# Two transformer layers in one launch: padded keys cleared on another engine, layer norms in two halves, another order of tiles in SBUF, scatters behind the first decays

## The chip, the cores and the metric

The kernel runs on one core of a Trainium2 chip. The engines of that core work side by side, each with an instruction queue taken strictly in order: PE (TensorE, matrix products and transposes, with PEld for its weight loads), DVE (VectorE), ACT (ScalarE), POOL (GpSimd) and SP (SyncE, which here only issues DMAs). POOL issues DMAs too: those that convert types, and the indirect ones that gather or scatter rows. Semaphores tie the queues together. SBUF is the memory on the chip, PSUM the small one that PE writes to. The metric is the time of one launch in microseconds (us) on the device.

## The reference, cut to what matters

T = 1024 tokens of width D = 256 go through two layers. Each is a layer norm, a token mixer, a mixture of experts, and a residual sum of the mixer times the gated experts.

```python
x = L0_attn_x
xn = _layernorm(x, axis=-1)
s = _L0_attn_ref(xn, wq, wk, wv, wo)            # 32 heads of width 8, 8 kv heads, causal softmax
g = _silu(_L0_ffn_ref(xn, gate, gate_up, down)) # 32 experts, 4 per token
x = x + s * g
xn = _layernorm(x, axis=-1)
s = _L1_attn_ref(xn, W_qkv, W_z, W_b, W_a, conv_w, dt_bias, A_log, norm_w, W_out)
g = _silu(_L1_ffn_ref(xn, Wr, Wg, Wu, Wd))      # 8 experts, 2 per token
x = x + s * g

def _layernorm(x, axis=-1, eps=1e-05):
    m = jnp.mean(x, axis=axis, keepdims=True)
    v = jnp.var(x, axis=axis, keepdims=True)
    return (x - m) / jnp.sqrt(v + eps)

# inside _L1_attn_ref: a gated delta rule over time, 32 value heads on 16 key heads of width 128
S = S * jnp.exp(gt)[..., None, None]
kS = jnp.einsum('bhk,bhkv->bhv', kt, S)
S = S + bt[..., None, None] * kt[..., :, None] * (vt - kS)[..., None, :]
o = jnp.einsum('bhk,bhkv->bhv', qt, S)
```

## The kernel before, in words

Tokens lie in NT = 8 tiles of 128. The kernel is written with a tile framework: pools of named tiles, and a scheduler that orders each engine's instructions by priority (program order, shifted by `high_priority`) over a simulated time. A pool that takes the place of an earlier one comes after it. In the first layer's main loop the orders of PE and SP are written out by hand; elsewhere the scheduler decides.

**First layer, `l0_block`.** Pool `l0c` holds what lives through the layer, placed in the order in which the code names it: `qp`, `kp`, `vaug`, `ytok`, `maskm`, `xn` (later `fo`), `logits`, the padded queries `qaugs`, keys `kaug` and `kzs`, then `xr`, `wo` and the plan. `kzs` are two tiles of [128, 4, 1024] that hold each head's keys in 32 rows of their own with zeros around them; POOL clears them once (L272), and SP later writes the rows (L408). `layer_norm` (L74) takes statistics of all eight tiles on DVE (L79, L80), then one reciprocal square root of all (L81, `rsqrt` at L50: eleven small DVE instructions), then scales all eight (L84). `transpose_split` (L87) turns `xn` on PE, four tiles at a time, with ACT keeping the rounded high part (L95) and DVE the rest (L96); its outer loop runs over the two halves of D, its inner loop over the two halves of T. Then eight projections of three product terms each (`mm3`, L69 to L71) with copies by ACT (L284 to L287). The weights come in raw by SP and rounded by POOL (`split_weights`, L47, L48), and POOL subtracts (L49). `moe.clear` (L135) fills the experts' input `l0xs` in DRAM with zeros from the tile `zero`. The loop then runs row maxima (L421, L423, L427), attention (L487, L491, L493) and expert blocks; the experts' results are gathered row by row by POOL (L222), and the tail (from L540) forms `x1` (L548 to L551).

**Second layer, `l1_block`.** Its constants are in pool `l1c`: `xnh` and `xnl` of 8 KB a partition each, then `tri_l`, `cw` and small ones. SP stores `x1` (L602) and loads `cw` (L610), `nw` (L613), clears `l1xs` (L135), loads `dt`, `ea` and the weights `wba` of the gates (L47). Layer norm and transposes follow (L1107, L1109), the products `ba` (L1118), the decays' exponents, and the routing plan (`Blocks.plan`), whose tiles lie in pool `l1a`. Pool `mp` (four `m` tiles) takes the place of `l1a`. Eight groups of heads follow, as generators that a string of letters steps through: K, Q, V are projections with a convolution on DVE (L681) and SiLU on ACT; P (`pre`) makes the eight decays of a group (`decay`: POOL selects `b` at L729, PE L731, ACT exp L733; then PE `pkk` L751, DVE products L762 into `m`, POOL select L771) and inverts the triangular blocks (DVE L791 and L793, then PE and ACT); R is the recurrence (L874 to L923); O the output (L964 to L983); F the expert blocks, which hold one `m` tile and one `v` tile from their first to their twelfth block. P has a priority 3000 instructions ahead of its place. `table` ties exps and SiLUs of ACT into windows.

Before the string `START` is run, eight loads `xt` (SP, L1160, from the stored `xn`; four buffers `kd`, which R uses too) and sixteen indirect DMAs on POOL (`moe.scatter`, L215) put the tokens into the experts' input `l1xs`. The sixteen scatters wait for the plan's `to` (L200).

Of the kernel before, what the change touches and what calls it, by code (L numbers as in the profile page):

```python
# [8 lines left out]
F32 = mybir.dt.float32  # L9
FR = mybir.dt.float32r  # L10
BF = mybir.dt.bfloat16
AF = mybir.ActivationFunctionType
ALU = mybir.AluOpType
# [6 lines left out]
T, D = 1024, 256  # L20
NT = T // 128
KT = D // 128


def f32(ap):
    return ap.bitcast(F32)
# [26 lines left out]
def rsqrt(nc, pool, out, x, n):  # L53

    I32 = mybir.dt.int32
    y = pool.tile([128, n], F32, tag="rsy", name="rsy")
    t = pool.tile([128, n], F32, tag="rst", name="rst")
    nc.vector.tensor_scalar(t.bitcast(I32), x.bitcast(I32), 1, None, ALU.logical_shift_right)
    nc.vector.tensor_scalar(y.bitcast(I32), t.bitcast(I32), -1.0, float(0x5F3759DF), ALU.mult, ALU.add)
    for i in range(3):  # L60
        nc.vector.tensor_tensor(t, y, y, ALU.mult)
        nc.vector.scalar_tensor_tensor(t, t, -0.5, x, ALU.mult, ALU.mult)
        nc.vector.scalar_tensor_tensor(out if i == 2 else y, t, 1.5, y, ALU.add, ALU.mult)
# [10 lines left out]
def layer_norm(nc, c, pool, x, xn):  # L74
    st = pool.tile([128, NT, 6], F32, tag="lnst", name="lnst")
    mv = pool.tile([128, NT, 2], F32, tag="lnmv", name="lnmv")
    rs = pool.tile([128, NT], F32, tag="lnrs", name="lnrs")
    for t in range(NT):
        nc.vector.bn_stats(st[:, t, :], x[:, t, :])  # L79
        nc.vector.bn_aggr(mv[:, t, :], st[:, t, :])  # L80
    nc.vector.tensor_scalar(rs, mv[:, :, 1], 1e-5, None, ALU.add)  # L81
    rsqrt(nc, pool, rs, rs, NT)
    for t in range(NT):
        nc.vector.tensor_scalar(xn[:, t, :], x[:, t, :], mv[:, t, 0:1], rs[:, t : t + 1], ALU.subtract, ALU.mult)  # L84


def transpose_split(nc, c, ps, tag, xn, hi, lo):  # L87

    for k in range(KT):
        for h in range(2):  # L90
            p = ps.tile([128, 4, 128], F32, tag=tag, name="ptr")
            for j in range(4):
                nc.tensor.transpose(p[:, j, :], xn[:, 4 * h + j, k * 128 : (k + 1) * 128], c.ident)
            sl = slice(512 * h, 512 * h + 512)
            nc.scalar.copy(hi[:, k, sl], p.rearrange("p a b -> p (a b)"))  # L95
            nc.vector.tensor_tensor(lo[:, k, sl], p.rearrange("p a b -> p (a b)"), f32(hi[:, k, sl]), ALU.subtract)  # L96
# [23 lines left out]
class Blocks:  # L120
# [91 lines left out]
    def scatter(self, tc, t, x):  # L212

        for k in range(self.K):
            ins = self.nc.gpsimd.indirect_dma_start(out=self.xs[:, :], out_offset=bass.IndirectOffsetOnAxis(ap=self.to[:, t, k : k + 1], axis=0),  # L215
                                                    in_=x, in_offset=None).ins
            for other in self.scatters:
                tc.declare_no_dep(ins, other, reason="different rows")
            self.scatters.append(ins)

    def gather(self, t, k, y):
        self.nc.gpsimd.indirect_dma_start(out=y, out_offset=None, in_=self.ys[:, :],  # L222
# [3 lines left out]
def l0_block(ctx, tc, c, x_d, wq, wk, wv, wo, gate, gup, dproj, x1, dbg=None):  # L226
    nc = tc.nc
# [4 lines left out]
    const = ctx.enter_context(tc.tile_pool(name="l0c", bufs=1))  # L232
    small = ctx.enter_context(tc.tile_pool(name="l0s", bufs=2))

    qp = const.tile([128, NT, 256], F32, name="qp")
    kp = const.tile([128, NT, 64], F32, name="kp")
    vaug = const.tile([128, NT, NKV, 32], F32, name="vaug")
# [4 lines left out]
    logits = const.tile([128, NT, NE], F32, name="logits")  # L242
    dram = ctx.enter_context(tc.tile_pool(name="l0d", bufs=1, space=bass.MemoryType.DRAM))
    moe = Blocks(nc, dram, "l0", NE, 4, per=2)
    qaugs = [const.tile([128, NT, 4, 32], FR, tag=f"qaug{i}", name=f"qaug{i}") for i in range(2)]
    kaug = const.tile([128, NT, 4, 32], FR, tag="kaug", name="kaug")


    kzs = [const.tile([128, 4, T], FR, tag=f"kz{i}", name=f"kz{i}") for i in range(2)]
    for q in qaugs:  # L250
        nc.vector.memset(f32(q), 0.0)
    nc.vector.memset(f32(kaug), 0.0)
# [4 lines left out]
    with tc.tile_pool(name="l0a", bufs=1) as pa, tc.tile_pool(name="l0ap", bufs=2, space=PSUM) as pp:  # L257
        x = pa.tile([128, NT, D], F32, name="x")
        xnh = pa.tile([128, KT, T], FR, name="xnh")
        xnl = pa.tile([128, KT, T], FR, name="xnl")  # L260
        zero = pa.tile([128, D], F32, name="zero")
        nc.vector.memset(zero, 0.0)
        nc.sync.dma_start(x, x_d.rearrange("(t p) d -> p t d", p=128))
        NW = NH * HD + 2 * NKV * HD + NE
        loads = []
        off = 0
        for w, n in ((wq, 256), (wk, 64), (wv, 64), (gate, 32)):
            loads.append((lambda t, o=off, n=n: t[:, :, o : o + n], w.rearrange("(k p) n -> p k n", p=128)))
            off += n
        wh, wl = split_weights(nc, pa, "wqkv", [128, KT, NW], loads)  # L270
        for kz in kzs:
            nc.gpsimd.memset(f32(kz), 0.0)  # L272
        layer_norm(nc, c, small, x, xn)
        transpose_split(nc, c, pp, "ptr", xn, xnh, xnl)
        nc.gpsimd.memset(maskm, 0.0)

        nc.gpsimd.affine_select(maskm, maskm, [[-1, 896]], ALU.is_ge, -1e30, base=384, channel_multiplier=1)
        moe.clear(zero)
        for t in range(NT):
            p = pp.tile([128, NW], F32, tag="pq", name="pq")  # L280
            for k in range(KT):
                ts = slice(t * 128, t * 128 + 128)
                mm3(nc, p, (xnh[:, k, ts], xnl[:, k, ts]), (wh[:, k, :], wl[:, k, :]), k == 0, k == KT - 1)
            nc.scalar.copy(qp[:, t, :], p[:, 0:256])  # L284
            nc.scalar.copy(kp[:, t, :], p[:, 256:320])
            nc.scalar.copy(vaug[:, t, :, 0:8], p[:, 320:384].rearrange("p (h d) -> p h d", d=8))
            nc.scalar.copy(logits[:, t, :], p[:, 384:416])  # L287
# [221 lines left out]
    streams = {"M": row_maxima(), "A": attend(), "F": experts()}  # L509
# [9 lines left out]
    with tc.manual_schedule(engines={mybir.EngineType.PE, mybir.EngineType.SP}):  # L519
# [4 lines left out]
        for u in range(steps):  # L524
# [4 lines left out]
            f = n * max(0, min(f1, u + 1) - f0) // (f1 - f0) - n * max(0, min(f1, u) - f0) // (f1 - f0) if u < f1 else 1  # L529
            if u == 4:  # L530
                f = 1
# [45 lines left out]
NB = {'k0': 4, 'k1': 4, 'q0': 2, 'q1': 3, 'v': 8, 'm': 4, 'b': 3, 'd': 13, 'yh': 1, 'yl': 1, 'gz': 2, 'w': 3, 'S': 3, 'kd': 4, 'bv': 3, 'W': 1, 'bt': 1, 'tmp': 1, 'wr': 1, 'st': 1, 'ct': 1}  # L577
OR, KD, SP = 'Pool', 'ACT', True
GPRIO = 2000
EARLY = 'KK'  # L580
START = 'UPPPPPPPPPPPPVVVVQQUPPPPKKFFFFFFFFFFFFU'
STEP = 'OPPPPRPROPOPRPVRVPOURPVRPRPPKKQPPRPQVU'
LAST = 'RROORRFFROOFFRFFRFFRFFR'

# [1 line left out]
def l1_block(ctx, tc, c, x1, wqkv, wz, wb, wa, convw, dtb, alog, normw, wout, wr, wg, wu, wd, out, x1_done=lambda: None):  # L586
    nc = tc.nc
# [4 lines left out]
    const = ctx.enter_context(tc.tile_pool(name="l1c", bufs=1))  # L592
# [6 lines left out]
    xnd = dram.tile([T, D], F32, name="xnd")  # L599
    moe = Blocks(nc, dram, "l1", NE, 2)  # L600
# [17 lines left out]
    gs = const.tile([128, NT, NG, 2, 4], FR, name="gs")  # L618
# [23 lines left out]
    def do_silus():  # L642
        while silus:
            d = silus.pop(0)
            table("silu", nc.scalar.activation(d, d, AF.Silu))

    def table(kind, ins):

        if not WINDOWS:
            return  # L650
        if kind != win[0]:
            win[0], win[1], win[2] = kind, win[2], []
        for before in win[1]:
            tc.add_manual_dep(ins.ins, before.name, mybir.DependencyInfo(mybir.DependencyClass.NoSync, mybir.DependencyReason.DATA),
                              reason="table sets")
        win[2].append(ins.ins)

    def load_w(src, cols):
# [65 lines left out]
    def decay(g, cc):  # L724

        p = ps("pe", [128, 512])
        for i in range(2):
            b = rc.tile([128, 4, 128], FR, tag="b", name="b", bufs=NB["b"])
            nc.gpsimd.affine_select(b, f32(gs)[:, cc, g, i, :, None].to_broadcast([128, 4, 128]), [[0, 4], [1, 128]], ALU.is_ge, 0.0,  # L729
                                    base=0, channel_multiplier=-1)  # L730
            nc.tensor.matmul(p, tri_l, b.rearrange("p a b -> p (a b)"), start=(i == 0), stop=(i == 1))  # L731
        d = rc.tile([128, 4, 128], F32, tag="d", name="d", bufs=NB["d"])
        table("exp", nc.scalar.activation(d.rearrange("p a b -> p (a b)"), p, AF.Exp))  # L733
        return d
# [331 lines left out]
    def flush():  # L1066
        while True:
# [3 lines left out]
    streams = {"K": all_groups(proj_k), "P": all_groups(pre), "V": all_groups(proj_v), "Q": all_groups(proj_q),  # L1071
               "R": all_groups(recs), "O": all_groups(outp), "F": ffn(), "U": flush()}
# [9 lines left out]
    with tc.tile_pool(name="l1a", bufs=1) as pa, tc.tile_pool(name="l1ap", bufs=2, space=PSUM) as pp:  # L1082
# [6 lines left out]
        zero = pa.tile([128, D], F32, name="zero")  # L1089
        nc.vector.memset(zero, 0.0)  # L1090
        moe.clear(zero)
        xn = pa.tile([128, NT, D], F32, name="xn")
        ba = pa.tile([128, NT, 72], F32, name="ba")
        g = pa.tile([128, NT, NV], F32, name="g")
# [60 lines left out]
    for k in "RB":  # L1155
        pools[k] = ctx.enter_context(tc.tile_pool(name="p" + k, bufs=PBUFS[k], space=PSUM))

    for t in range(NT):
        xt = rc.tile([128, D], F32, tag="kd", name="xt", bufs=NB["kd"])
        nc.sync.dma_start(xt, xnd[128 * t : 128 * t + 128, :])  # L1160
        moe.scatter(tc, t, xt)


    run(START)
    for g in range(NG):
# [4 lines left out]
    for t in range(NT):  # L1170
        for k in range(2):
            tag = ("kd", "bv")[k]
# [71 lines left out]
```

## Time and profile before

| what | us |
|---|---|
| median of three runs | 1928.91 |
| lowest and highest run | 1925.61, 1929.6 |
| the profiled execution | 1922.61 |
| span of its trace | 1920.6 |
| PE busy in it | 1581.3 (82%) |
| DVE busy | 1339.8 (70%) |
| ACT busy | 1053.3 (55%) |
| POOL busy | 754.5 (39%) |

Times inside the text are counted from the start of the span. The first layer runs to about 522 us, where the last `x1` tile is added (L551). From 522 to about 720 us the second layer starts up; from about 850 to 1700 us one group of heads follows another in a period of 144 us, and the rest is the end of the last group, the last expert blocks and the output.

How its views are read: the timeline gives start, duration, engine, line, operation, tile written and tiles read, the number of merged instructions, and in brackets the idle time before it and what ended it. A group of merged instructions has one duration from the first start to the last end. The table of windows gives for each stretch its length, the busy time of each engine with the number of instructions, the TensorE clock that was granted (1.00 is full), the DMA share and GB/s. A line of the waits gives the waiting instruction, what it waited for, the time in all, how often, and the longest.

### The profile page before, as it was taken

The page shows a single profiled execution, that of the slowest core. Times are in us where ns is not written, and L with a number is a line of the kernel's source. Part 1 is how long each engine was busy: PE and PEld are TensorE (multiplying, and loading weights), DVE is VectorE, ACT ScalarE, POOL GpSimd, SP SyncE. Part 2 cuts the span into 40 slices and gives each one's busy share as a digit, 9 for nine tenths or more (in the row PEclk, how much of TensorE's full clock was granted, in tenths as well). Part 3 has the DMA queues.
Part 4 walks back from the last instruction along what each step waited for, and adds up shares of the span by engine and source line. Part 5 has one row for each costly group of instructions (what it writes and reads, how often), then busy time and mean ns, then how long its engine had stood idle before and what let it go on. Part 6 is the DMA issues. An engine that isn't in the chain of part 4 may idle for free. (4 is left out here: it accounts for less than half of the span.)

```text
span 1920.6 us, 34083 instructions
## 1 busy us (share of the span) xinstructions
PE 1581.3 (82%) x11566; PEld 1207.1 (63%) x11566; DVE 1339.8 (70%) x3833; ACT 1053.3 (55%) x2844; POOL 754.5 (39%) x949
## 2 busy tenths in 40 slices
PE   4789988989656699889799799799799799879854
PEld 3446666666444377667677577677677677658643
DVE  6675565555659827947977978978978977963332
ACT  2345545544423356646677566576576566646632
POOL 4051000000616425157347347347347347433263
PEclk9799999999858679979999999999999999989977
DMA  8024444441362421012103203103103103204535
GB/s 261 12 86 129 127 120 126 131 133 60 104 147 78 116 69 52 17 35 61 39 24 67 44 24 72 39 24 72 39 24 72 39 23 72 63 16 98 139 88 124
DMA packets 149755, 147.28 MB, mean 77 GB/s; under 512 B 22013, under 2 KB 137037, under 8 KB 149581
## 3 DMA queue, kind: packets, MB, share of 16 engines
q1 hardware_dynamic: 115853, 97.15, 17.1%
q0 software_dynamic: 33728, 47.96, 11.9%
q8 instruction: 92, 1.51, 0.3%
q14 instruction: 82, 0.67, 0.1%
HBM read 91.59 MB, written 49.28 MB: 73 GB/s over the span
## 5 line engine op out<-in xcount | busy, mean ns | idle before, releaser
L493 ACT ACTIVATE pe<-p 128x1024 f32<-128x1024 f32 (+1 forms) x192 | 154.6, 813 | 113.6 <-PE p L491 83.5
L427 DVE CUSTOM_DVE_ANT_0 junk<-p,maskm 128x128 bf16<-128x128 f32 (+3 forms) x256 | 125.2, 489 | 59.7 <-PE p L421 48.9
L69 PE MATMUL pc<-xnh,wl 128*128 128x512 f32 x256 | 118.5, 464 | 42.1 <-DVE last L687 12.3
L893 PE MATMUL pw<-bv,m 128*128 128x128 f32 x512 | 92.4, 300 | 71.5 <-DVE bv L885 67.6
L681 DVE SCALAR_TENSOR_TENSOR v<-pc,cw,v 128x511 f32<-128x511 f32 (+2 forms) x192 | 140.3, 740 | 2.6 <-ACT v L678 1.7
L893 PEld LDWEIGHTS pw<-bv,m 128*128 128x128 f32 x512 | 74.8, 194 | 100.2 <-DVE bv L885 87.0
L421 PE MATMUL p<-kz,qT 128*128 128x512 f32 (+3 forms) x384 | 116.7, 396 | 19.7 <-DMA kz<-kT 11.5
L907 POOL TENSOR_TENSOR S<-S,eC 128x256 f32<-128x256 f32 x96 | 59.6, 621 | 182.9 <-PE pk L887 147.8
L487 PE MATMUL p<-q,kz 128*128 128x512 f32 (+3 forms) x384 | 122.6, 404 | 6.8 <-ACT pe L493 2.2
L923 ACT ACTIVATE sq<-v 128x128 bf16<-128x128 f32 x256 | 77.3, 307 | 88.8 <-DVE v L918 78.7
L49 POOL TENSOR_TENSOR wl<-wr,wh 128x512 fp32r<-128x512 f32 x68 | 88.4, 1301 | 94.5 <-DMA wh<-in_L_attn_W_z_dram 24.2
L895 ACT ACTIVATE W<-pw,cf 128x128 f32<-128x128 f32 x256 | 79.9, 365 | 60.0 <-PE pw L893 58.4
L965 DVE SCALAR_TENSOR_TENSOR gz<-gz,pz 128x512 f32<-128x512 f32 x64 | 43.8, 685 | 92.6 <-ACT gz L964 92.4
L71 PE MATMUL pc<-xnl,wh 128*128 128x512 f32 x256 | 107.4, 420 | 0.0
L70 PE MATMUL pc<-xnh,wh 128*128 128x512 f32 x256 | 107.2, 419 | 0.0
L874 ACT ACTIVATE kd<-pt,eR 128x128 f32<-128x128 f32 x256 | 79.8, 361 | 45.7 <-PE pt L865 44.3
L423 DVE TENSOR_REDUCE mx<-p 128x2 f32<-128x1024 f32 x64 | 77.8, 1223 | 32.7 <-PE p L421 32.1
L793 DVE TENSOR_TENSOR X<-X,Ad 128x31 f32<-128x31 f32 (+15 forms) x248 | 97.6, 394 | 3.8
L791 DVE TENSOR_TENSOR Ad<-Ab,X 128x31 f32<-128x31 f32 (+15 forms) x248 | 93.4, 376 | 3.3
L421 PEld LDWEIGHTS p<-kz,qT 128*128 128x128 f32 x384 | 66.1, 202 | 40.8 <-ACT pe L493 10.1
L973 POOL TENSOR_TENSOR yl<-gz,yh 128x512 fp32r<-128x512 f32 x64 | 84.0, 1315 | 19.3 <-ACT yh L972 19.1
L69 PEld LDWEIGHTS pc<-xnh,wl 128*128 128x128 f32 x256 | 51.9, 203 | 62.3 <-DVE last L687 12.8
(356 smaller groups left out, 5062.8 us busy)
## 6 DMA issues: line engine op xcount, KB each, us to landing
sTd<-st POOLq DMA_DIRECT2D x32, 512.0 KB, 6.4
gw<-_L_ffn_gate_up_proj_dram SPq DMA_DIRECT2D x64, 192.0 KB
l0xs<-zero SPq DMA_DIRECT2D x1, 8320.0 KB
xb<-l0xs SPq DMA_DIRECT2D x32, 256.0 KB
l0ys<-y SPq DMA_DIRECT2D x32, 256.0 KB
wh<-in_L_attn_W_qkv_dram POOLq DMA_DIRECT2D x32, 256.0 KB, 3.1
wr<-in_L_attn_W_qkv_dram SPq DMA_DIRECT2D x32, 256.0 KB
dw<-in_L_ffn_down_proj_dram SPq DMA_DIRECT2D x64, 96.0 KB
```

What stands on the lines that cost most here:

```text
L49: nc.gpsimd.tensor_tensor(lo, raw, f32(hi), ALU.subtract)
L69: nc.tensor.matmul(out, al, bh, start=start, stop=False)
L70: nc.tensor.matmul(out, ah, bh, start=False, stop=False)
L71: nc.tensor.matmul(out, ah, bl, start=False, stop=stop)
L421: nc.tensor.matmul(p[:, h - h0, :n], qT[:, 128 * i : 128 * i + 128], kz[:, h, 512 * j : 512 * j + n], start=True, stop=True)
L427: nc.vector.tensor_tensor_reduce(junk[:, :n], p[:, h - h0, :n], maskm[:, o : o + n], 1.0, -3e38, ALU.add, ALU.max, accum_out=mx[:, i, h, 0:1])
L487: nc.tensor.matmul(p[:, h - h0, :n], kz[:, h, 128 * kt : 128 * kt + 128], q2[:, 512 * qb + o : 512 * qb + 512], start=True, stop=not diag)
L493: nc.scalar.activation(e[:, :, :n], p[:, :, :n], AF.Exp, scale=SC)
L681: nc.vector.scalar_tensor_tensor(d[:, o:512], p[:, 0 : 512 - o], cw[:, n, i : i + 1], d[:, o:512], ALU.mult, ALU.add)
L791: nc.vector.tensor_tensor(t, Ab[:, j, j + 1 : 32, None].to_broadcast([128, n, m]), X[:, j, None, 0:m].to_broadcast([128, n, m]), ALU.mult)
L793: nc.vector.tensor_tensor(X[:, j + 1 : 32, 0:m], X[:, j + 1 : 32, 0:m], t, ALU.add)
L893: nc.tensor.matmul(pw[:, 0, i, :], M[:, 4 * (cc % 4) + 2 * j + i, :], bv[:, i, :], start=True, stop=True)
```

## The change

Five edits, in four parts of the kernel.

1. `kzs` are cleared by ACT, with copies from the tile `zero`, one for each of the four heads of each tile, and no longer by POOL.
2. `layer_norm` works on four tiles at a time: statistics, reciprocal square root and scaling of the first half, then of the second. It serves both layers.
3. `transpose_split` has its loops exchanged: both halves of D for the first half of T, then for the second. It serves both layers and the first layer's tail.
4. In `l0c` the tiles `kzs`, `qaugs`, `kaug` are named first, so they lie at the start of the pool.
5. The second layer's loads `xt` and scatters become a stream S that `START` steps through after the first eight P steps, and each scatter is put behind the last `b` select of group 0's eighth decay in POOL's order (an order without a wait). The manual dependency that `table` already used is named `order_only`.

```diff
-    for t in range(NT):
-        nc.vector.bn_stats(st[:, t, :], x[:, t, :])
-        nc.vector.bn_aggr(mv[:, t, :], st[:, t, :])
-    nc.vector.tensor_scalar(rs, mv[:, :, 1], 1e-5, None, ALU.add)
-    rsqrt(nc, pool, rs, rs, NT)
-    for t in range(NT):
-        nc.vector.tensor_scalar(xn[:, t, :], x[:, t, :], mv[:, t, 0:1], rs[:, t : t + 1], ALU.subtract, ALU.mult)
+    H = NT // 2
+    for h in range(2):
+        hs = slice(H * h, H * h + H)
+        for t in range(H * h, H * h + H):
+            nc.vector.bn_stats(st[:, t, :], x[:, t, :])
+            nc.vector.bn_aggr(mv[:, t, :], st[:, t, :])
+        nc.vector.tensor_scalar(rs[:, hs], mv[:, hs, 1], 1e-5, None, ALU.add)
+        rsqrt(nc, pool, rs[:, hs], rs[:, hs], H)
+        for t in range(H * h, H * h + H):
+            last = nc.vector.tensor_scalar(xn[:, t, :], x[:, t, :], mv[:, t, 0:1], rs[:, t : t + 1], ALU.subtract, ALU.mult)
+    return last
 
 def transpose_split(nc, c, ps, tag, xn, hi, lo):
-    for k in range(KT):
-        for h in range(2):
+    for h in range(2):
+        for k in range(KT):
...
+    kzs = [const.tile([128, 4, T], FR, tag=f"kz{i}", name=f"kz{i}") for i in range(2)]
+    qaugs = [const.tile([128, NT, 4, 32], FR, tag=f"qaug{i}", name=f"qaug{i}") for i in range(2)]
+    kaug = const.tile([128, NT, 4, 32], FR, tag="kaug", name="kaug")
     qp = const.tile([128, NT, 256], F32, name="qp")
...
-    qaugs = [const.tile([128, NT, 4, 32], FR, tag=f"qaug{i}", name=f"qaug{i}") for i in range(2)]
-    kaug = const.tile([128, NT, 4, 32], FR, tag="kaug", name="kaug")
-
-
-    kzs = [const.tile([128, 4, T], FR, tag=f"kz{i}", name=f"kz{i}") for i in range(2)]
...
         for kz in kzs:
-            nc.gpsimd.memset(f32(kz), 0.0)
+            for h in range(4):
+                nc.scalar.copy(kz[:, h, :].rearrange("p (a b) -> p a b", b=D), zero[:, None, :].to_broadcast([128, T // D, D]))
...
-START = 'UPPPPPPPPPPPPVVVVQQUPPPPKKFFFFFFFFFFFFU'
+START = 'UPPPPPPPPSSSSSSSSPPPPVVVVQQUPPPPKKFFFFFFFFFFFFU'
...
+    def order_only(ins, before):
+        tc.add_manual_dep(ins, before.name, mybir.DependencyInfo(mybir.DependencyClass.NoSync, mybir.DependencyReason.DATA), reason="order")
+
+    last_b = [None]
...
-            nc.gpsimd.affine_select(b, f32(gs)[:, cc, g, i, :, None].to_broadcast([128, 4, 128]), [[0, 4], [1, 128]], ALU.is_ge, 0.0,
-                                    base=0, channel_multiplier=-1)
+            last_b[0] = nc.gpsimd.affine_select(b, f32(gs)[:, cc, g, i, :, None].to_broadcast([128, 4, 128]), [[0, 4], [1, 128]], ALU.is_ge, 0.0,
+                                                base=0, channel_multiplier=-1)
...
-    for t in range(NT):
-        xt = rc.tile([128, D], F32, tag="kd", name="xt", bufs=NB["kd"])
-        nc.sync.dma_start(xt, xnd[128 * t : 128 * t + 128, :])
-        moe.scatter(tc, t, xt)
-
+    def scatters():
+        for t in range(NT):
+            xt = rc.tile([128, D], F32, tag="kd", name="xt", bufs=NB["kd"])
+            nc.sync.dma_start(xt, xnd[128 * t : 128 * t + 128, :])
+            for ins in moe.scatter(tc, t, xt):
+                order_only(ins, last_b[0].ins)
+            yield
+
+    streams["S"] = scatters()
```

## The prediction

> **Which views, in which order.** The busy tenths in 40 slices of 48 us come first, then the timeline of the first 60 us, the table of windows, and the waits from 522 to 700 us. The chain of waits does not help: it names only the store and load of `sTd` at 1% each and breaks off near the end.
>
> ```profile
> PE   4789988989656699889799799799799799879854
> ...
> DVE  6675565555659827947977978978978977963332
> ...
> POOL 4051000000616425157347347347347347433263
> PEclk9799999999858679979999999999999999989977
> ```
>
> From slice 17 (about 850 us) on the rows repeat every three slices, 144 us a group; seven groups follow each other rigidly, so what a group starts earlier the kernel ends earlier. The weak places are slice 0 and slices 10 to 14 (480 to 720 us), where PE falls to 5 or 6. The change touches just these.
>
> ```profile
> 5.11 6.98 POOL L272 MEMSET kz<- 128x4096 f32 x2
> ...
> 6.68 6.39 DVE L561 CAST identb<-ident 128x128 bf16<-128x128 f32 x1
> ...
> 14.01 1.96 POOL L49 TENSOR_TENSOR wqkvl<-wqkvr,wqkvh 128x832 fp32r<-128x832 f32 x1
> ...
> 14.46 2.43 DVE L81 TENSOR_SCALAR lnrs<-lnmv 128x8 f32<-128x8 f32 x1
> ...
> 19.17 2.67 DVE L84 TENSOR_SCALAR xn<-x,lnmv,lnrs 128x256 f32<-128x256 f32 x8
> ...
> 40.75 2.52 SPq L408 DMA_DIRECT2D kz<-kT  x4
> ```
>
> A 128x128 cast takes 6.39 us and a tensor_scalar over 8 numbers 2.43 us. The first ends (13.07) after the Pool's kz clears (12.09) and maskm clear (12.88); the second (16.89) after the Pool's subtraction of wqkvl (15.97) and a select. The same small ops alone take 0.17 to 0.3. So DVE stands behind the Pool twice, about 4.4 us (eight statistics at 0.33 from 6.86 would end at 9.5, not 13.88) and 2.2 us.
>
> ```profile
> 30.00:35.00 5.00, 5.00 (x27) 4.70 (x26) 0.00 (x0) 2.94 (x18) 0.00 (x0) 1.00 1.09 387
> 35.00:36.00 1.00, 0.09 (x1) 0.00 (x0) 0.14 (x1) 0.87 (x6) 0.00 (x0) 1.00 0.52 182
> 36.00:40.00 4.00, 1.47 (x13) 1.48 (x14) 3.15 (x24) 2.30 (x8) 2.27 (x3) 1.00 0.00 0
> ...
> 590.00:602.00 12.00, 5.65 (x24) 3.95 (x23) 11.92 (x55) 3.07 (x6) 4.46 (x7) 0.92 0.20 54
> 602.00:650.00 48.00, 33.50 (x110) 23.44 (x108) 42.70 (x130) 21.38 (x41) 40.20 (x54) 0.78 0.41 128
> 650.00:678.00 28.00, 18.63 (x74) 10.12 (x76) 25.00 (x67) 4.61 (x13) 1.94 (x2) 0.50 0.34 98
> 678.00:715.00 37.00, 36.58 (x492) 29.23 (x489) 5.40 (x14) 19.58 (x52) 6.26 (x12) 0.72 0.20 58
> ```
>
> The columns are PE, PEld, DVE, ACT, POOL, the granted clock, DMA share, GB/s. The DMAs run full until 35.5 us: that is the clear of `l0xs` (8.3 MB). Later, 602 to 650 is a stretch of DVE and Pool, 650 to 678 of DVE alone (the inversion of group 0) with PE at half clock, 678 to 715 of PE alone.
>
> ```profile
> POOL tri_l L606 <- DVE x L551: 6.3, 1, 6.3
> ...
> PE pq L71 <- POOL wbal L49: 8.7, 1, 8.7
> ...
> PE pe L731 <- POOL b L729: 5.1, 4, 2.1
> ```
>
> **1. kz cleared by ScalarE.** Removed: 6.98 us of Pool. Added: 8 ACT copies of 128x1024; the nearest rows are the casts of L386 (1.00 to 1.01 us), so 8.0 us, from 6.6 (when `zero` is set) to 14.6. ACT does nothing there until 21.1; kz is first written at 40.75. What can be late is the first cast of xnh, which stands behind them on ACT: cost 0 if the first half is transposed after 14.6, at most 1.5 if at 13.1.
>
> **2. Halves, first layer.** DVE unblocked: statistics of half 0 from 6.86, 4 x 0.33, aggregates 0.3, L81 0.2, eleven rsqrt ops at 0.20 = 2.2, four xn at 0.33: 12.2. The second half adds the same 5.4: 17.6, of which 2.4 (twelve small ops) is new work. Against 21.84 before that is 4.2 earlier for the whole and 9.6 for half 0. The weights of wqkvh land near 10.9, so the Pool's subtraction now runs 10.9 to 12.9, over the xn of half 0, and may hold them as it held L81: 0 to 2.4 us; I take 2, since both are tensor_scalars beside the same instruction. So xn ends at 19.6. From the last xn before to the end of the eight projections took 13.3 us; with four tiles of 1.13 us done meanwhile it is about 8.8, so they end near 28.5 instead of 35.1; kT is ready 5.5 us later, at 34 instead of 40.7. The kz loads then meet the clear of `l0xs`, which does not end before 35.5. Bounds: they share the queues with it and land at 36; they wait for it, need 512 KB at 380 KB/us after it, and land at 37; or DVE orders the second half ahead of the first splits, kT comes at 36.5 and they land at 40.2. Before, they landed at 44.5. Gain 4.3 to 8.5; I take 6, between the last two, since SP issues kz on the same queue as the clear. Below: 2, if the first casts too are late.
>
> [...]
>
> [...] No row yet has kz behind the clear.
>
> **3. Halves, second layer.** xn ends 2.4 us later, 534.4 for 531.97. It is covered: the `ba` products wait for wbal until 547.4 (row above, 8.7 us), a load behind the 10 us of nw, the l1xs clear and dt on SP. Without that cover it costs 2.4. But PE may now order the first products ahead of the second half's eight transposes (2.6 us), and then stands at wbal with these behind it, as do `xnl` on DVE and its casts. 0 to 4; I take 1. The second layer's transposes and the tail's (L540) only change order: the tail is paced by gathers at 1.25 us each (0 to -1, taken as 0).
>
> **4. Tiles by end.** tri_l lies 16 KB into l1c, over vaug (10 to 18 KB into l0c), which attention has done with at 502. Yet it waits for the last x1 addition (row above), which reads xr, 81 KB into l0c. The wait is for the whole pool, so the new order frees nothing: 0 is taken. Were it by tile, l1c would lie over kz and cw could go 20 us earlier; of that the wbal chain could keep about 10 (the issue of nw), which I leave to the low end.
>
> **5. Scatters.** Sixteen indirect DMAs at 0.97 + 0.30 = 20.3 us of Pool, and eight xt loads on SP, go behind the sixteenth `b`. Nothing is removed. Group 0's m products wait in both kernels for the plan's tiles until 602.5. Then decays 2 to 7 end at 642.9: 6.4 us each, with Pool 40.2 of 48 us busy and PE waiting for b. Without scatters between, one decay is pkk 0.6, two junk 0.6, reciprocal and cf 0.4, four products at 0.34 = 1.4, and hops: 3.5 to 4. So they end near 604.6 + 6 x 3.8 = 627, 15 us earlier, and the inversion with them; convolutions of DVE slide behind it, into 678 to 715, where DVE has 31 us free. Against it: the scatters end near 645 instead of 624.8, so the second layer's first twelve expert blocks (their stores lie at 647 to 751, 9.5 us each) start 20 us later, and xt loads hold SP and the kd buffers as long. Some four blocks at 3 to 4 us of PE leave the stretch in which PE idles. So 15 less 0 to 15: gain 0 to 15. I take 9, since DVE, not PE, is the engine full on both sides of it.
>
> **Sum.** -6 + 1 + 0 - 9 = -14. The profiled execution took 1922.61 (span 1920.6 and 2 around it): 1908.6. It lies 6.3 under the median; from 1928.91 the forecast is 1915.
>
> **Rivals.** *Only the start pays* (steps 1 to 3, scatters neutral because DVE conserves its 113 us of work between 557 and 680): -5, 1924. For it: DVE is busy 42.7 of 48 us. Against: PE does wait for b. *Nothing arrives*: a later transfer or order takes back the 5 us, 1929; for it, the row of clocks has half-speed stretches that move; against, a rigid PE order behind. *Slower*: the expert blocks hold one of the four m buffers. Group 1's second m needs that one, or group 0's first m, which its fourth W pair frees at about 749. If the twelfth block ends 20 us late and the buffer planned for group 1 is the one that it holds, the inversion of group 1 (762) waits for it: +20, less 6 at the start, +14, 1943; it decides from the point where the twelfth block ends after 762. For it: blocks end at 751 today, just beside 749. Against: group 0's m comes free too, and earlier than today. That a part does not do what it says is step 4.
>
> **Chances.** Both gains 0.50 (1915, own range 1904 to 1922); start only 0.22; nothing 0.10; slower 0.18. About 0.2% (3.9 us) is what can be told from no change; a little of the start-only case falls within it: faster 0.70, same 0.12, slower 0.18. Low end: 7.5 + 15 and part of step 4's bound, 1899. High: leaving out the worse half of the slow case, 1934.
>
> **What would show it.** identb's cast under 0.5 us; xn of half 0 done before 15; kz landing at 37 to 40; tri_l still behind x L551; m of decay 7 near 627 (less the start's shift), first W of group 0 (691.8) some 10 to 20 earlier. Wrong if the inversion of group 1 begins later than 762, or if ACT's or DVE's order puts the second half before the first splits.

## The result, and the profile after

| | before | after |
|---|---|---|
| median of six runs each, same chip | 1929.26 | 1949.43 |
| lowest and highest run | 1925.01, 1937.37 | 1944.05, 1953.37 |
| profiled execution | 1922.61 | 1951.38 |
| its span | 1920.6 | 1949.7 |
| granted TensorE clock, mean over the span | 0.918 | 0.901 |

The ratio is 1.0098, with a 95% interval of 1.0071 to 1.0125: slower by 1%, against a forecast of 0.7% faster.

The busy tenths of the kernel after, in 40 slices of 49 us, show the first difference:

```profile
PE   4789899898566498798798799798898899789864
...
DVE  6666566555669637949959958969968978954432
...
POOL 2060000002525433167257247257247338334262
PEclk9899999998777599899989989999889989889977
```

Counted from 0, slice 13 (634 to 682 us) has PE at 4 and the clock at 5, the kernel before 6 and 6. From slice 17 to 35, the steady groups, the row of clocks has seven 8s; before it had one. The start of the first layer is as it was meant to be. The timeline of the first 45 us:

```profile
6.62 7.67 ACT L278 CAST kz<-zero 128x1024 fp32r<-128x1024 f32 x8 [4.51 <-DVE zero L267]
6.68 0.24 DVE L567 CAST identb<-ident 128x128 bf16<-128x128 f32 x1
6.86 2.65 DVE L82 BATCH_NORM_STATS2 lnst<-x 128x6 f32<-128x256 f32 x8
...
11.51 2.01 DVE L62 SCALAR_TENSOR_TENSOR rst<-rst,lnrs 128x4 f32<-128x4 f32 x2
11.56 1.94 POOL L49 TENSOR_TENSOR wqkvl<-wqkvr,wqkvh 128x832 fp32r<-128x832 f32 x1 [3.27 <-DMA wqkvh<-in_L_ffn_gate_dram]
...
14.23 2.67 DVE L87 TENSOR_SCALAR xn<-x,lnmv,lnrs 128x256 f32<-128x256 f32 x8
...
36.19 2.52 SPq L414 DMA_DIRECT2D kz<-kT  x4
```

The cast takes 0.24 us instead of 6.39, eight ACT copies take 7.67 us, `kz` is loaded from 36.19 instead of 40.75. The "x2" of the lines with [128, 4] operands and the "x8" of L87 say something else: the scheduler ran both halves of the layer norm side by side, operation by operation. There is no early first half. The store of `x1` that opens the second layer is issued at 517.6 us (522.5).

The start of the second layer, as windows (columns as before) and as waits:

```profile
590.00:602.00 12.00, 8.27 (x19) 5.95 (x19) 11.83 (x48) 1.37 (x2) 3.21 (x4) 0.50 0.18 45
602.00:650.00 48.00, 19.41 (x81) 14.59 (x79) 36.41 (x128) 19.26 (x35) 37.66 (x51) 0.71 0.30 90
650.00:678.00 28.00, 18.21 (x120) 10.08 (x123) 23.55 (x56) 5.07 (x13) 5.78 (x7) 0.50 0.35 101
678.00:715.00 37.00, 37.00 (x480) 30.36 (x471) 6.39 (x23) 22.06 (x61) 7.58 (x14) 0.82 0.24 67
```

```profile
PE pxt L1028 <- DVE X L804: 22.8, 1, 22.8
PE pq L71 <- POOL wbal L49: 8.5, 1, 8.5
DVE Ab L796 <- POOL Ad L38: 8.2, 1, 8.2
```

From 602 to 650 us PE does 19.4 us instead of 33.5 and DVE 36.4 instead of 42.7, while POOL is as busy as before (37.7, was 40.2). The waits of 22.8 and 8.2 us are new. In the first, PE stands before the first expert block (`pxt`, its transposes) until 654.3 us; before, that block began at 630.8. The profile names DVE's `X`, but `pxt` reads `fin`, whose rows SP loads from 652.1 us on, after the last scatter (issued until 650.7, before 624.8). In the second, `Ad` are POOL's copies of the diagonal blocks of `m`; `Ab` is the DVE transpose that opens a group's inversion. The timeline of that stretch, DVE and POOL:

```profile
627.53 1.11 DVE L773 SCALAR_TENSOR_TENSOR m<-pkk,cf,d 128x128 f32<-128x128 f32 x4
628.11 0.96 POOL L219 DMA_INDIRECT l1xs<-xt,to  x1 [0.30 <-issue]
629.38 0.96 POOL L219 DMA_INDIRECT l1xs<-xt,to  x1 [0.30 <-issue]
630.64 0.96 POOL L219 DMA_INDIRECT l1xs<-xt,to  x1 [0.30 <-issue]
631.61 0.65 POOL L782 TENSOR_SCALAR_AFFINE_SELECT d<-d 128x512 f32<-128x512 f32 x1
...
638.77 0.96 POOL L219 DMA_INDIRECT l1xs<-xt,to  x1 [0.30 <-issue]
639.73 0.65 POOL L782 TENSOR_SCALAR_AFFINE_SELECT d<-d 128x512 f32<-128x512 f32 x1
640.32 0.62 POOL L38 TENSOR_SCALAR_AFFINE_SELECT Ad<-m 32x512 f32<-32x512 f32 x1
641.54 1.92 POOL L38 TENSOR_SCALAR_AFFINE_SELECT Ad<-m 32x512 f32<-32x512 f32 x3 [0.60 <-DMA l1xs<-xt,to]
643.49 2.04 DVE L796 STREAM_TRANSPOSE Ab<-Ad 128x1024 f32<-128x1024 f32 x1 [8.19 <-POOL Ad L38]
```

The last product of decay 7 starts at 628.3 us (642.9 before). But the copies that the inversion needs stand in POOL's queue behind scatters and selects, until 643.5. The inversion starts 3.2 us earlier than before (646.7), less than the 4.9 us that the start of the layer had brought.

One group in the steady stretch, from one first state row `W` to the next. Before, then after:

```profile
1421.00:1568.00 147.00, 128.90 (x1097) 104.29 (x1090) 122.58 (x335) 95.64 (x291) 78.37 (x100) 0.97 0.21 44
```

```profile
1441.00:1597.00 156.00, 135.65 (x1068) 112.19 (x1066) 128.22 (x345) 97.87 (x292) 79.41 (x101) 0.90 0.22 45
```

The same work takes PE 6.8 us longer at a clock of 0.90 instead of 0.97, and the group 9 us longer. The forecast took this period for fixed.

### The profile page after: what moved, and what is told of

It is laid out like the page before. It is cut to its first block, busy times and chain, and to the rows that moved or that the text cites. A ratio compares the mean times of both kernels' runs of the same rounds, so it can differ in the third digit from the quotient of the medians.

```text
span 1949.7 us, 34096 instructions
## 1 busy us (share of the span) xinstructions
PE 1595.3 (82%) x11566; PEld 1228.7 (63%) x11566; DVE 1346.6 (69%) x3857; ACT 1063.7 (55%) x2852; POOL 749.4 (38%) x947
## 4 chain that ended last, share of the span: by engine, by line
PE 49%; DVE 29%; ACT 7%; issue 6%; DMA 5%; POOL 2%; SPq 1%; DVEq 0%; ACTq 0%; POOLq 0%
DVE v L692 4%; PE p L427 3%; PE av L453 3%; PE pw L904 3%; PE p L493 3%; DVE Ad L802 3%; DVE X L804 2%; PE pg L337 2%; PE pm L854 2%; PE ps L911 2%; PE pmw L926 2%; DVE bv L896 2%; PE pc L69 2%; PE pk L898 2%; PE pt L876 2%
## 5 line engine op out<-in xcount | busy, mean ns | idle before, releaser
L433 DVE CUSTOM_DVE_ANT_0 junk<-p,maskm 128x128 bf16<-128x128 f32 (+3 forms) x256 | 125.2, 489 | 60.0 <-PE p L427 49.5
L69 PE MATMUL pc<-xnh,wl 128*128 128x512 f32 x256 | 123.8, 484 | 38.1 <-DVE last L698 12.3
L904 PE MATMUL pw<-bv,m 128*128 128x128 f32 x512 | 98.6, 313 | 63.5 <-DVE bv L896 63.1
L692 DVE SCALAR_TENSOR_TENSOR v<-pc,cw,v 128x509 f32<-128x509 f32 (+2 forms) x192 | 141.1, 740 | 6.9 <-ACT v L689 6.1
L918 POOL TENSOR_TENSOR S<-S,eC 128x256 f32<-128x256 f32 x96 | 65.3, 680 | 202.1 <-PE pk L898 115.3
L904 PEld LDWEIGHTS pw<-bv,m 128*128 128x128 f32 x512 | 80.1, 206 | 92.4 <-DVE bv L896 86.5
L885 ACT ACTIVATE kd<-pt,eR 128x128 f32<-128x128 f32 x256 | 80.2, 361 | 67.2 <-PE pt L876 62.5
L802 DVE TENSOR_TENSOR Ad<-Ab,X 128x31 f32<-128x31 f32 (+15 forms) x248 | 97.5, 393 | 3.7
L984 POOL TENSOR_TENSOR yl<-gz,yh 128x512 fp32r<-128x512 f32 x64 | 86.7, 1355 | 29.9 <-ACT yh L983 28.8
L896 DVE SCALAR_TENSOR_TENSOR bv<-pk,eG,bv 128x128 f32<-128x128 f32 x224 | 68.2, 342 | 36.3 <-ACT bv L886 27.4
```

The costliest lines, as they stand in the source:

```text
L69: nc.tensor.matmul(out, al, bh, start=start, stop=False)
L433: nc.vector.tensor_tensor_reduce(junk[:, :n], p[:, h - h0, :n], maskm[:, o : o + n], 1.0, -3e38, ALU.add, ALU.max, accum_out=mx[:, i, h, 0:1])
L692: nc.vector.scalar_tensor_tensor(d[:, o:512], p[:, 0 : 512 - o], cw[:, n, i : i + 1], d[:, o:512], ALU.mult, ALU.add)
L802: nc.vector.tensor_tensor(t, Ab[:, j, j + 1 : 32, None].to_broadcast([128, n, m]), X[:, j, None, 0:m].to_broadcast([128, n, m]), ALU.mult)
L896: nc.vector.scalar_tensor_tensor(bv[:, i, :], pk[:, 0, i, :], eG[:, cc, h0 + i : h0 + i + 1], bv[:, i, :], ALU.mult, ALU.add)
L904: nc.tensor.matmul(pw[:, 0, i, :], M[:, 4 * (cc % 4) + 2 * j + i, :], bv[:, i, :], start=True, stop=True)
```

## Where the time went

Five points of a trace divide the span: the store of `x1` (SP), the last expert block of the first twelve (its first PE transpose, `pxt`), the transposes `Ab` that open the inversions of groups 0 and 1, and the last row `W`. "Half" is the time within the fourth column during which TensorE had half its clock. All in us, from the profiled execution of each kernel; the labels are those of the experiments below.

| kernel | x1 to Ab of group 0 | x1 to Ab of group 1 | Ab 1 to last W | half | last W to end | order of the steady groups |
|---|---|---|---|---|---|---|
| before | 124.2 | 234.8 | 1076.9 | 95.6 | 86.2 | its own |
| after | 125.9 | 242.7 | 1091.7 | 160.4 | 97.7 | another |
| e1 | 125.9 | 238.8 | 1080.0 | 105.8 | 86.0 | as before |
| e5 | 123.3 | 231.8 | 1083.3 | 116.1 | 86.0 | as before |
| e7 | 148.9 | 261.8 | 1077.5 | 95.6 | 85.8 | as before |
| e8 | 148.1 | 261.0 | 1067.8 | 71.7 | 85.3 | as before |
| e9 | 125.0 | 247.3 | 1084.0 | 109.2 | 86.1 | as before |
| e10 | 116.4 | 251.3 | 1080.5 | 105.8 | 85.6 | as before |
| e12 | 125.6 | 233.9 | 1086.4 | 119.5 | 86.1 | as before |
| e2 | 125.2 | 238.8 | 1094.5 | 153.6 | 84.1 | another |
| e3 | 123.3 | 236.5 | 1081.3 | 129.7 | 97.0 | another |
| e4 | 127.9 | 236.7 | 1093.6 | 133.1 | 86.7 | another |
| e6 | 127.6 | 240.7 | 1084.8 | 109.2 | 85.2 | that of e4 |
| e11 | 124.0 | 241.5 | 1095.0 | 157.0 | 95.0 | that of after |

After against before, in the two profiled executions: 4.9 us gained until the store of `x1`, then 7.9 lost until group 1's inversion (242.7 - 234.8), 14.8 in the groups (1091.7 - 1076.9) and 11.5 at the end (97.7 - 86.2). That makes 29.3, and the spans lie 29.1 us apart. The medians lie 20.2 us apart, since the profiled run of before was 6.7 us under its median and that of after 2 us over.

These are single executions, and the columns differ between executions of one order too. The four traces with before's order and the scatters in their old place (before, e1, e5, e12) spread from 231.8 to 238.8 us in "x1 to Ab of group 1", the eight with before's order from 1067.8 to 1086.4 in "Ab 1 to last W" and from 85.3 to 86.2 in "last W to end". After lies outside all three, and so does e11 with the same steady order (241.5, 1095.0, 95.0); the sizes 7.9 and 14.8 are rough.

The change touches no work of the steady groups. What differs there is the order of the instructions. Take each engine's from 30 us behind the store of `x1` on and count from the end: of PE's 8767, 2420 have the same operation and tiles in the same place after as before, of DVE's 2845 only 592. The scheduler orders each engine over a simulated time, and a shifted start sends it another way. Clearing the padded keys on ACT alone, or the new layout alone, leaves the second layer's order as it was (in e1 and e12 all of DVE's 2845 are in their place). So the first theory (A) was that the other order costs the time; the rivals were that the scatters cost it where they stand (B), or the halves themselves (C).

## The experiments

They ran on chips that differ: the kernel before has a median of 1973.49 us beside e1 to e4, 1925.94 beside e5 to e8, 1974.85 beside e9 to e12. Every ratio is against the kernel before on the same chip. A difference between two ratios (e4 and e5, e1 and e6, e1 and e9 or e11) goes across chips; that a ratio is the same on each of them was not tried. On one chip, e6 lies 0.0060 above e5, and e11 0.0088 above the kernel before.

**Parts alone.** e1 has the kz copies and nothing else. e2 has the scatters' edit and nothing else. e3 is the change without the scatters' edit. e4 is e1 with halves in the first layer alone: no line of the second layer differs from before.

```diff
 # e1
-            nc.gpsimd.memset(f32(kz), 0.0)
+            for h in range(4):
+                nc.scalar.copy(kz[:, h, :].rearrange("p (a b) -> p a b", b=D), zero[:, None, :].to_broadcast([128, T // D, D]))
 # e4, beside that
-        layer_norm(nc, c, small, x, xn)
-        transpose_split(nc, c, pp, "ptr", xn, xnh, xnl)
+        layer_norm_halves(nc, c, small, x, xn)
+        transpose_split_halves(nc, c, pp, "ptr", xn, xnh, xnl)
```

> Only the clear of the padded keys goes to ScalarE; every engine's order of instructions in the second layer is that of the kernel before. Theory A (the changed kernel loses because the order of the second layer's work came out differently, not through any edit's own cost): 4 to 5 us faster, near 1924, with groups 3 to 6 still 144 us apart. Theory B (the scatters' move costs) and theory C (the halves cost) expect the same. If the copies on ScalarE cost something themselves: 1929 or more.

> Only the scatters are put behind the first decays. Theory B: this edit carries the loss, 1945 to 1955, and the loss begins with the expert blocks before 850 us. Theory A: the group 0 decays end 12 to 15 us earlier as in the changed kernel and what is won or lost in time lies after 988 us, in the period of the groups (144 us before, up to 156 after), with more half clock where it is longer; 1915 to 1955, the sign open. Theory C: 1929 or faster.

> Keys cleared on ScalarE, layer norms by halves, transposes by halves; scatters where they were. Theory B: 1923 to 1925. Theory C: 1944 or more. Theory A: five us ahead at the end of the first layer, and then whatever period the new order gives; some loss against 1924, between 1920 and 1950.

> Keys on ScalarE, and the halves only in the first layer's layer norm and its transposes; the code of the second layer and of the tail is untouched. Its second layer still comes out in another order of instructions. Theory A: the gain of 5 us is there at the start of the second layer, but the groups' period may differ from 144 us though no line of that layer was edited; 1918 to 1945. Theories B and C (for the second layer's halves): 1924 with a period of 144 us.

Measured: e1 0.9962 (0.9944 to 0.9981), e2 1.0088 (1.0061 to 1.0114), e3 1.0070 (1.0038 to 1.0103), e4 1.0035 (1.0010 to 1.0060). The padded keys carry the whole gain of the start: in e1 the last `xn` ends at 16.96 us and the kz loads begin at 35.1, after 16.90 and 36.2, in e4 16.87 and 37.2, before 21.84 and 40.7. The halves add nothing and make the kernel slower by 0.7% although they end before the second layer begins. That speaks for A. e2 loses 0.9% in yet another order of the groups (1094.5 us, 153.6 at half clock), so it fits A and B alike. e3 shows that the scatters are not needed for a loss; its end is 10.8 us longer than before's. But none of these tells the order from the thing that brought it about.

**The order held, and swapped.** The next kernels hold the second layer's instructions, engine by engine, in a recorded order, by dependencies that only order and wait for nothing:

```diff
+def pin_order(nc, tc, base, table):
...
+    by = {ins.name: ins for ins in nc.all_instructions()}
+    for seq in lists:
+        for a, b in zip(seq, seq[1:]):
+            tc.add_manual_dep(by["I-%d" % (base + b)], "I-%d" % (base + a),
+                              mybir.DependencyInfo(mybir.DependencyClass.NoSync, mybir.DependencyReason.DATA), reason="order")
```

> The kernel of e4 (padded keys cleared by ScalarE, halves in the first layer only), with one thing more: on each engine the second layer's 11593 instructions are held in the order that the kernel before has. Theory A (what loses time is the other order of the second layer's instructions, which the changed start brings about): the loss is gone, ratio as of the padded keys alone, 0.996 (0.994 to 0.999), and TensorE's half-clock time from 850 to 1700 us falls from 102 us to some 75. Theory C (the halves themselves, or the earlier start of the second layer, lose it): the ratio stays at 1.0035 (1.001 to 1.006).

> The converse: the kernel of e1 (padded keys alone, ratio 0.996), with the second layer's instructions held in the order that e4 has. No halves, no moved scatters. Theory A: it loses what e4 lost, ratio 1.003 (1.001 to 1.006), with the half-clock time from 850 to 1700 us near 100 instead of 75. Theory C: it stays at 0.996.

Measured: e5 0.9980 (0.9959 to 1.0000), e6 1.0040 (1.0019 to 1.0061). With before's order e4 loses its loss (1.0035 to 0.9980); with e4's order e1 loses its gain (0.9962 to 1.0040). Order alone, with the same instructions, makes 0.6 to 0.8%, some 11 to 15 us. C falls for the first layer's halves. What holding an order costs by itself is bounded by e5 alone: it lies 0.0018 above e1, within the intervals. The clock followed as expected in e5 only: from 850 to 1700 us it stood at half for 71.7 us (102.4 in e4), but in e6 for 71.2 (75.1 in e1). In e6's trace the loss against e5 is before group 1's inversion (240.7 against 231.8), in e4's it is in the groups (1093.6 against 1080.0 in e1). So the order's price is shown by the ratios, and the place where one order pays it is not always the same.

**The whole change with the order held.**

> The whole change, with the second layer's instructions held in the order of the kernel before from the layer norm's end on, all but the 16 scatters and their 8 loads, which the change puts behind the first half's selects. Theory A with the forecast's own terms: the order's cost is gone, and of the forecast gain at least the start's 5 us stay: ratio 0.990 to 0.998. Theory A without any gain of the moved scatters (the second half's copies of group 0 wait behind them): 0.996. Theory B (the scatters cost time where they now stand, by buffers or by POOL's queue): 1.003 or more, though the order is kept.

> Padded keys by ScalarE and the moved scatters, without the halves, order of the second layer held as in the kernel before but for the scatters. Against e7 it tells what the halves are worth once the order can't change: theory A with halves worth nothing (e1 had the whole gain of the start): the same as e7 within 0.2%. If halves help or hurt the second layer's start, it differs from e7 by that. Theory B: 1.003 or more.

Measured: e7 1.0118 (1.0087 to 1.0148), e8 1.0103 (1.0073 to 1.0133). Against theory A alone: the order is before's, and they lose as much as the whole change. The waits of e7 from 618 to 668 us name it:

```profile
PE pxt L1028 <- DMA fin<-l1xs: 27.9, 1, 27.9
DVE fgz L1038 <- ACT fgz L1037: 27.5, 1, 27.5
POOL b L740 <- PE pe L742: 8.5, 1, 8.5
```

In before's order PE's first expert block stands ahead of group 0's last two decays. Its rows come through the scatters, so all of PE stands 27.9 us behind them, POOL's last selects behind PE, and the inversion of group 0 starts at 148.9 instead of 124 us after the store of `x1`. From there on all is nearly rigid: the first rows `W` of e7's eight groups lie 28.5, 29.3, 29.3, 26.1, 28.9, 25.6, 25.5 and 25.3 us behind those of e5, and its span 25.2. So the forecast's premise holds where the order holds, but its gain comes back as a wait. The halves are worth nothing here either (e7 against e8).

**Only the steady groups held.** e9 keeps the change's own order of group 0, scatters and expert blocks, and holds before's order from about 750 us on. e10 also ties the scatters behind the last `Ad` copy. e11 is the converse of e9: e1 with the steady order of the whole change. e12 is the layout alone.

```diff
 # e10, beside e9's table
-START = 'UPPPPPPPPSSSSSSSSPPPPVVVVQQUPPPPKKFFFFFFFFFFFFU'
+START = 'UPPPPPPPPPSSSSSSSSPPPVVVVQQUPPPPKKFFFFFFFFFFFFU'
...
-                pool_copy(nc, Ad[s, 16 * h : 16 * h + 16], G.m[h][s, :, s])
+                last_b[0] = pool_copy(nc, Ad[s, 16 * h : 16 * h + 16], G.m[h][s, :, s])
```

> The whole change, its own order of the second layer up to about 750 us (group 0's decays, scatters, inversion and expert blocks as the change has them), and from there on each engine held in the order of the kernel before. Theory A (the loss is the order of groups 1 to 7): the 690 us of the first state row of group 0 (692 before) is kept to the end, ratio 0.997 to 1.001. Theory B (what loses is where the scatters stand, or the expert blocks that come 11 us later): the ratio stays at 1.005 or more.

> As e9, with the 16 scatters tied behind the last copy of group 0's diagonal blocks (L795) instead of behind the last decay's select (L740). If the 15 us that the decays gain are given back because POOL's queue has scatters ahead of these copies, the inversion of group 0 starts at 634 to 640 us instead of 646 and, the order being kept, the ratio is 0.991 to 0.996. If the later expert blocks (their rows come with the scatters, some 15 us later still) decide, group 0 gains and the end does not: 0.998 or more.

> The converse of e9: padded keys alone (ratio 0.996), scatters and layer norms as before, with each engine held from about 762 us on in the order that the whole change has. Theory A: it loses as the whole change does, ratio 1.003 to 1.012, and the loss arises in groups 3 to 6. Theory B: it stays at 0.996 to 0.999.

> The first layer's tiles laid out by their end, and nothing else. No engine's order changes. The forecast put this at nothing: 1.000 (0.998 to 1.002). If the other addresses cost or gain by themselves, it lies outside.

Measured: e9 1.0064 (1.0039 to 1.0088), e10 1.0055 (1.0034 to 1.0077), e11 1.0088 (1.0057 to 1.0118), e12 1.0001 (0.9979 to 1.0024). Both theories are right in part, and neither alone.

- e11 has no moved scatter and no halves, and loses as much as the whole change: the order that the scheduler made for it costs 1.3% against e1, with 157.0 us of half clock (105.8) and 9.0 us more at the end.
- e9 has before's steady order, 109.2 us of half clock and before's end, and still loses. The place is group 1's inversion. Timelines of e1, of e9 and of the kernel after around it:

```profile
787.32 0.38 PE L1018 MATMUL pxt<-ident,fin 128*128 128x128 f32 x2
...
789.80 2.16 DVE L763 SCALAR_TENSOR_TENSOR m<-pkk,cf,d 128x128 f32<-128x128 f32 x8 [2.24 <-PE pg L1025]
...
802.81 2.06 DVE L786 STREAM_TRANSPOSE Ab<-Ad 128x1024 f32<-128x1024 f32 x1
```

```profile
796.98 0.38 PE L1028 MATMUL pxt<-ident,fin 128*128 128x128 f32 x2
...
799.47 2.16 DVE L773 SCALAR_TENSOR_TENSOR m<-pkk,cf,d 128x128 f32<-128x128 f32 x8 [2.23 <-PE pg L1035]
...
812.50 1.97 DVE L796 STREAM_TRANSPOSE Ab<-Ad 128x1024 f32<-128x1024 f32 x1
```

```profile
744.43 0.75 PE L904 MATMUL pw<-bv,m 128*128 128x128 f32 x4 [0.77 <-DVE bv L896]
...
745.22 2.16 DVE L773 SCALAR_TENSOR_TENSOR m<-pkk,cf,d 128x128 f32<-128x128 f32 x8 [0.58 <-PE pw L904]
...
753.81 0.38 PE L1028 MATMUL pxt<-ident,fin 128*128 128x128 f32 x2
...
760.25 2.12 DVE L796 STREAM_TRANSPOSE Ab<-Ad 128x1024 f32<-128x1024 f32 x1
```

The products at 789.80 (e1), 799.47 (e9) and 745.22 us (after) are the first into the second of group 1's two `m` tiles. What they wait for is that tile's buffer. In e1 the `pkk` that they read has ended 12.9 us earlier (776.9), and DVE stands 2.2 us until the twelfth block's last `pg` (789.76). That `pg` is the last reader of `fin`, and in the code `fin` is one of the four `m` tiles (`mp.tile(..., tag="m", name="fin")`). `Ab` follows, 15.5 us after the block's transposes. The same wait of 2.2 us and the same 15.5 to 15.6 us stand in all eight traces with before's order, before's own among them. The blocks begin when the scatters have landed, so in this order a later scatter is a later group 1, and everything behind it.

In the kernel after (and in e2 and e11) the same products wait instead for `pw` of group 0's fourth `W` pair, the last reader of group 0's first `m` tile. They start 227.6 us after the store of `x1`, before 221.8: 5.8 of the 7.9 us. The late blocks themselves they do not wait for; the twelfth's `pg` ends only at 756.25.

- e10 shows both at once. Its inversion of group 0 starts 116.4 us after `x1` instead of 125.0: the give-back at POOL is real, 8.6 us. And its twelfth block, with group 1, comes still later (251.3 instead of 247.3). What group 0 gains the end does not see.

The price of the order (e11 against e1, 0.0126) and that of the later blocks (e9 against e1, 0.0102) are together more than the whole change's loss (0.0136 against e1). They need not add: group 1 waits for the blocks in e9 and for group 0's tile in after and e11, so e9's wait is not met there. In e11 the first block starts as early as in e1 (108.1 and 108.8 us after `x1`), but the held order brings the twelfth at 235.1 us, as in after (236.2), and not at 223.3. How the loss of the change divides between the two stays open, and so does which feature of its order costs the time in the groups and at the end.

The padded keys alone (e1) are faster than both kernels, by 0.38% against before.

## Why the prediction was wrong, point by point

- *kz on ScalarE, first-layer halves (-6):* near in size, 4.9 us, but all of it from the kz copies. The loads were to begin at 34 us and began at 36.2. The forecast itself named as a sign of error that DVE's order mixes the halves; it did. The 2 us taken for `xn` beside POOL's subtraction came at L62: two of its instructions, 0.28 us where POOL runs nothing beside them (10.92 and 13.84), took 2.01 (11.51 to 13.52) beside the subtraction (11.56 to 13.50). The 6 also had the kz loads wait for the clear of `l0xs` on the queue they share. The trace of after shows no such wait: the clear had all but ended when they were issued at 36.19 (387 GB/s from 30 to 35 us, 177 in the next, none from 36.5 to 37), and from 37 to 38 they moved 131.
- *Halves, second layer (+1):* from the store of `x1` to the second `ba` copy 34.3 us, 34.6 before. Nothing, at the low bound.
- *Tiles by end (0):* right, e12 (1.0001).
- *Scatters (-9), the step that failed:* "So they end near 604.6 + 6 x 3.8 = 627, 15 us earlier, and the inversion with them". The decays ended 14.6 us earlier, 4.9 of them brought from the start. The inversion did not come with them: POOL's scatters stand ahead of the `Ad` copies (8.2 us of wait). And the cost of the later expert blocks was bounded at 0 to 15 us against the gain, as PE work that moves, with no loss possible. They did start 23.5 us later (654.3 against 630.8, where 20 were expected), but what they cost is not work. They hold an `m` buffer that group 1 needs (e9), and in the change's own order group 1 waits for another one, of group 0. The first `W` of group 0 came 1.9 us earlier (689.9, before 691.8), where 10 to 20 were named as the sign, and the time from `x1` to group 1's inversion grew by 7.9 us where 9 were to be gained.
- *The premise:* "seven groups follow each other rigidly, so what a group starts earlier the kernel ends earlier". True for a fixed order (e7 against e5), but the change gives the scheduler another start, and it made another order: 14.8 us in the groups, 11.5 at the end. The forecast had "a later transfer or order takes back the 5 us" as the rival *nothing arrives* and priced it at 0; a new order can cost more than the gain. At the end, 177 PE instructions fall in the stretch from the last `W` on, 155 before.
- *The slower rival (1943)* was nearest to the result and had part of the cause: expert blocks 20 us late, and group 1's second `m` waiting for the buffer of the blocks or for group 0's first `m`. Both waits are in the traces, the one in before's order, the other in after. Its condition was wrong: it counted from the twelfth block's store (762 us, 751 before), but `fin` is free at the last `pg` (744.3 before), and the kernel before already waited 2.2 us for it. Nor did its sign show, an inversion of group 1 later than 762: it began at 760.3, since the start had come 4.9 us earlier. The 14.8 us in the groups and 11.5 at the end it did not have; that its number came near is in part luck.

## What to carry to other kernels

In a kernel whose order a scheduler makes from simulated times, a small edit at the start is a new draw of the whole order behind it. Compare the instruction orders of the two programs before forecasting a shift, and hold the old order to tell the edit from the draw. When work is moved behind other work on one queue, follow what it feeds to its last consumer: here the scatters' rows feed blocks that hold a buffer which the next group needs, so in before's order their place set group 1's start whatever group 0 gained.

## What the runs showed of the hardware

In the traces of before and after the granted clock is either full or half (0.5), and each stretch of either, but for the last of the trace, lasts a whole number of windows of 3.41 us. Of the 249 such windows that begin between 850 and 1700 us, 14 are at half clock before and 38 after. Of the windows at half clock 57% (before) and 34% (after) follow one in which PE was busy less than half the time; of those at full clock 1% and 2%. In the window ahead of one at half clock PE was busy 49% (before) and 59% (after) in the median, as the profile counts busy. From the first `W` of group 3 to that of group 6 (1134 to 1568 us before, 1135 to 1597 after) there are 5 such windows before and 25 after. Over the eight traces with before's order, the time from `Ab` of group 1 to the last `W` goes from 1067.8 us at 71.7 us of half clock to 1086.4 at 119.5: 0.39 us for each. So the half clock goes with the order's price and with the differences between executions. That it is the cause and not a sign of the order's other waits was not tried: a kernel that fills PE's sparse moments would tell.

The same code took longer on another chip in the first layer: the store of `x1` came at 564.0 us in e1 and at 516.9 in e6, whose first layer is e1's. About half of it lies between 100 and 200 us, where PE is busy for 67.2 us in e1 and 90.1 in e6. Why was not followed.
